# A four-layer graph network on one core: layer 0 reads the adjacency matrix by columns instead of by rows

## The chip, the core and the metric

The kernel runs on one core of a Trainium2 chip. The core has five engines that run side by side: PE (TensorE, matrix products and transposes), DVE (VectorE), ACT (ScalarE), POOL (GpSimd) and SP (SyncE, which here only issues DMAs). Each engine works through its own instructions in the order of the program and waits on semaphores for the others. The metric is the device time of one launch in microseconds (us); less is better.

## What is computed

x holds 2708 nodes of 128 features, adj is a sparse 2708 x 2708 matrix of float32 (some 17 entries a row, the diagonal always set). Four layers follow one another, each adding its result to x. Those that this change touches are the first two:

```python
# --- layer 0 ---
h = jnp.maximum(_layernorm(x), 0.0)
msg = jnp.matmul(adj.T, h)               # sum over rows of adj
inv_deg = 1.0 / adj.sum(axis=0)          # inf becomes 0
x = x + msg * inv_deg[:, None]
# --- layer 1 ---
h = jnp.maximum(_layernorm(x), 0.0)
s = h @ msg_w[:, :D].T
d = h @ msg_w[:, D:].T
messages = gelu(s[:, None, :] + d[None, :, :] + msg_b)
aggregated = jnp.einsum('ijd,ij->id', messages, adj)
new = jnp.concatenate([h, aggregated], -1) @ upd_w.T + upd_b
g = gelu(new) + h
x = x + layernorm(g) * ln_w + ln_b
# layer 2: adj @ h, then a GRU cell; layer 3: masked attention over adj
```

Layer 1 needs the messages only where adj is not zero, and the kernel uses that.

## The kernel before

The nodes lie in NT = 22 tiles of P = 128 rows (the last has TAIL = 20); GROUPS takes them four at a time, so there are six groups, the last with two tiles. For layer 1 the columns are cut into NB = 22 blocks of JB = 124, and each row's entries in a block are kept as a list of at most S = 8 values (`val`) and places (`col`).

**Layer 0** goes down adj by rows. `load_row_tile` reads 128 whole rows (1.35 MB) into one quarter of a set; two sets of four tiles are in use in turn. Each row tile is used four times:

- `list_row_tile` makes the lists on DVE: for every block a `max` (the eight largest, L283) and a `max_index` (their places, L285). Blocks that hold a part of the diagonal are first copied on POOL with the diagonal taken out (`near`). Row tiles from LATER = NT - 2 on list only those near blocks here; the others, `late_blocks`, are read again and listed three a period in layer 1 (`load_late`, `list_late`).
- `sign_sums` counts the entries of each row on ACT (L290), for a check at the end that no list ran over.
- `aggregate_rows` (PE, L297) adds h of this tile times the rows into six PSUM banks `accs`, one for each 512 columns, which hold the sums transposed and stay open over all 22 row tiles.
- `turn_blocks` transposes the tile's blocks on PE (L309). ACT copies each four of them out of PSUM, summing the columns on the way (L313), and SP writes the result to adjT in HBM, from which layer 2 reads.

The order is written out by hand (`manual_schedule`): after a set's first tile, each of the 22 steps j turns one block of the set and does a share of the products. The first four tiles of x are normalised by moments on DVE; the other 18 by sums on ACT (`sum_rows`, `sum_squares`), and a group's `normal_rows` comes one group ahead of its use.

When the last row tile is done, DVE counts the first four tiles' lists (L350 to L352), DVE and ACT copy the six banks to SBUF (L355), and five small DVE operations make the inverse degrees (L360 to L364).

**Layer 1** begins with an opening, also in an order by hand (the step list from L854 on). For each group `spread_sums` transposes the sums back (L791), `enter` adds them to x and takes moments (L800, L118 to L121), `rows` normalises (L127 to L131 on DVE, L137 on ACT), `turn_rows` transposes h (L155, L157), and `destinations` and `split_destinations` project it and split it in three bfloat16 parts (L826, L841 to L843). In between, the lists of row tiles 0, 1 and 2 pass through the steps that each tile needs: `rank` (L465), `select_rows` (DVE, L437), a shift by one row through DMA (L481), `finish_rows` (L487), `fetch` (L498), `place` (L511 to L532), `pass_on` (two DMAs, L564 and L566), `columns` (L574), `put_values` (POOL, L543).

Then `period(t)` runs for every tile: `combine` (PE, L625 and L629) builds the messages, ACT takes the Gelu, `gather` (L650) adds them up, while later tiles pass through the earlier steps. combine(0, 0) and the first gather mark the end of the opening. Layers 2 and 3 follow with code of their own.

The line that fixes the order in layer 0's inner loop is

```python
turn_blocks(gi, j)
now = len(steps) * (j + 1) // NT if gk == 4 else min(len(steps), j + 1)
```

Of the kernel before, what the change touches and what calls it, by code (L numbers as in the profile page):

```python
# [45 lines left out]
S = 8  # L46
# [14 lines left out]
def listed_layers(ctx: ExitStack, tc: tile.TileContext, x, adj, w, out, flag):  # L61
# [80 lines left out]
    def normalise(dst, src, t, k, func, name):  # L142

        rows = tiles_of(src, t, k)
        scale_rows(tiles_of(dst, t, k), rows, *factors(*moments(rows, name)), func)

# [12 lines left out]
    normalise(h, xs, 0, 4, AF.Relu, "n0")  # L159

# [6 lines left out]
    total = keep.tile([P, NT], F32, name="total")  # L167
# [27 lines left out]
    LATER = NT - 2  # L195
    AT_ONCE = 3
    late_blocks = []
    nc.gpsimd.memset(val[:, NT - 1, :, :], 0.0)
    nc.gpsimd.memset(col[:, NT - 1, :, :], 0.0)

    sumT = keep.tile([D, N], F32, name="hT1")
    hT = sumT
    with tc.tile_pool(name="l0c", bufs=1) as fix:
        offdiag = fix.tile([P, P], F32, name="offdiag")
        nc.vector.tensor_scalar(offdiag, ident, -1.0, 1.0, ALU.mult, ALU.add)
        sums = fix.tile([P, NT, len(GROUPS)], F32, name="sums")
        nc.gpsimd.memset(sums, 1.0)

        RT = NT - 4
        flat = fix.tile([P, 4, RT], F32, name="flat")
        shifts, ve, rstd, tmp = (flat[:, q, :] for q in range(4))

        def sum_rows(pool):
            for t in range(4, NT):
                junk = pool.tile([P, D], F32, name="junk")
                nc.scalar.activation(junk, xs[:, t, :], AF.Copy, accum_out=shifts[:, t - 4 : t - 3])
            nc.gpsimd.tensor_scalar(shifts, shifts, -1.0 / D, None, ALU.mult)

        def sum_squares(pool):
            for t in range(4, NT):
                junk = pool.tile([P, D], F32, name="junk")
                nc.scalar.activation(
                    junk, xs[:, t, :], AF.Square, bias=shifts[:, t - 4 : t - 3], accum_out=ve[:, t - 4 : t - 3]
                )
            nc.gpsimd.tensor_scalar(ve, ve, 1.0 / D, EPS, ALU.mult, ALU.add)
            nc.gpsimd.tensor_tensor(rstd, ve, minus_half[:, 0:RT], ALU.pow)
            nc.gpsimd.tensor_tensor(tmp, rstd, rstd, ALU.mult)
            nc.gpsimd.tensor_tensor(tmp, tmp, ve, ALU.mult)  # L230
            nc.gpsimd.tensor_scalar(tmp, tmp, -0.5, 1.5, ALU.mult, ALU.add)
            nc.gpsimd.tensor_tensor(rstd, rstd, tmp, ALU.mult)
            nc.gpsimd.tensor_tensor(shifts, shifts, rstd, ALU.mult)

        def normal_rows(g):
            t, k = GROUPS[g]
            scale_rows(tiles_of(h, t, k), tiles_of(xs, t, k), rstd[:, t - 4 :], shifts[:, t - 4 :], AF.Relu)

        with (
            tc.tile_pool(name="l0", bufs=2) as rows,  # L240
            tc.tile_pool(name="l0k", bufs=2) as pool,
            tc.tile_pool(name="l0t", bufs=8) as turned,
            tc.tile_pool(name="l0p", bufs=1, space=PSUM) as acc,
        ):
            accs = [acc.tile([P, CH], F32, name=f"acc{c}") for c in range(len(CHUNKS))]
            sets, marks = {}, {}

            def load_row_tile(n):
                gi, q, m = n // 4, n % 4, size(n)
                if q == 0:  # L250
                    sets[gi] = rows.tile([P, 4, N], F32, name="a")
                if m < P:
                    nc.gpsimd.memset(sets[gi][:, q, :], 0.0)
                nc.sync.dma_start(sets[gi][0:m, q, :], adj[n * P : n * P + m, :])

            def list_row_tile(n):

                m = size(n)
                a = sets[n // 4][:, n % 4, :]
                d0 = n * P  # L260
                b0 = d0 // JB
                b1 = (d0 + m - 1) // JB
                c0, c1 = b0 * JB, min((b1 + 1) * JB, N)
                near = pool.tile([P, 3 * JB], F32, name="near")
                nc.gpsimd.tensor_copy(near[:, 0 : c1 - c0], a[:, c0:c1])
                nc.gpsimd.tensor_tensor(
                    near[:, d0 - c0 : d0 - c0 + m], a[:, d0 : d0 + m], offdiag[:, 0:m], ALU.mult
                )
                marks[n] = pool.tile([P, P], F32, name="dg")
                nc.gpsimd.tensor_tensor(marks[n][:, 0:m], a[:, d0 : d0 + m], ident[:, 0:m], ALU.mult)  # L270

                def block(b):
                    if b0 <= b <= b1:
                        return near[:, b * JB - c0 : b * JB - c0 + width(b)]
                    return a[:, b * JB : b * JB + width(b)]

                blocks = [b for b in range(NB) if not b0 <= b <= b1] + list(range(b0, b1 + 1))
                if n >= LATER:
                    late_blocks.extend((n, b) for b in range(NB) if not b0 <= b <= b1)
                    blocks = range(b0, b1 + 1)  # L280
                for k in range(0, NB, 2):
                    for b in blocks[k : k + 2]:
                        nc.vector.max(val[:, n, b, :], block(b))  # L283
                    for b in blocks[k : k + 2]:
                        nc.vector.max_index(col[:, n, b, :], val[:, n, b, :], block(b))  # L285

            def sign_sums(n):
                m = size(n)
                sign = pool.tile([P, N], BF16, name="sign")
                nc.scalar.activation(sign, sets[n // 4][:, n % 4, :], AF.Sign, accum_out=total[:, n : n + 1])  # L290
                dg = marks.pop(n)[:, 0:m]
                nc.scalar.activation(dg, dg, AF.Copy, accum_out=own[:, n : n + 1])

            def aggregate_rows(n, ci):
                c, cw = CHUNKS[ci]
                m = size(n)
                nc.tensor.matmul(  # L297
                    accs[ci][:, 0:cw], h[0:m, n, :], sets[n // 4][0:m, n % 4, c : c + cw],
                    start=(n == 0), stop=(n == NT - 1),
                )  # L300

            def turn_blocks(gi, j):
                g0, gk = GROUPS[gi]
                i0, iw = span(g0, gk)
                k = size(j)
                p = bank("p_T")
                for q in range(gk):
                    m = size(g0 + q)
                    nc.tensor.transpose(  # L309
                        p[0:k, q * P : q * P + m], sets[gi][0:m, q, j * P : j * P + k], ident[0:m, 0:m]  # L310
                    )
                aT = turned.tile([P, CH], F32, name="aT")
                nc.scalar.activation(aT[0:k, 0:iw], p[0:k, 0:iw], AF.Copy, accum_out=sums[0:k, j, gi : gi + 1])  # L313
                nc.sync.dma_start(adjT[0:k, j, i0 : i0 + iw], aT[0:k, 0:iw])

            with tc.manual_schedule():
                for n in range(8):
                    load_row_tile(n)
                    if n == 1:
                        load_rest()  # L320
                for gi, (g0, gk) in enumerate(GROUPS):
                    steps = [(n, ci) for n in range(g0, g0 + gk) for ci in range(len(CHUNKS))]
                    ahead = gi == 0
                    for n in range(g0, g0 + gk):
                        if ahead:
                            for ci in range(len(CHUNKS)):
                                aggregate_rows(n, ci)
                        if n < 2:
                            list_row_tile(n)
                            sign_sums(n)  # L330
                            (sum_rows, sum_squares)[n](pool)
                    done = 0
                    for j in range(NT):
                        turn_blocks(gi, j)
                        now = len(steps) * (j + 1) // NT if gk == 4 else min(len(steps), j + 1)
                        for step in steps[done:now]:
                            if not ahead:
                                aggregate_rows(*step)
                        done = now
                        n = g0 + j // 5  # L340
                        if j % 5 == 1 and j // 5 < gk and n > 1:
                            list_row_tile(n)
                        if j % 5 == 3 and j // 5 < gk and n > 1:
                            sign_sums(n)
# [50 lines left out]
    with (  # L395
# [331 lines left out]
        def period(t, between=()):  # L727
# [5 lines left out]
            for k in range(GB):  # L733
# [45 lines left out]
                if k == 4:  # L779
                    load_late(t + 1)  # L780
# [957 lines left out]
```

## Time and profile before

| | us |
|---|---|
| median of 3 runs | 1064.76 (1064.54 to 1066.95) |
| the profiled execution | 1063.62 |
| its span, first to last instruction | 1061.8 |
| layer 0, to the last list on DVE | 205.3 |
| opening of layer 1, to the first gather | 205.3 to 290.5 |
| periods of layer 1, to the last gather | 290.5 to 609.0 |
| layers 2 and 3 | to the end |

Over the whole span PE is busy 87% of the time, DVE 77%, ACT 48% and POOL 43%; the mean granted TensorE clock is 0.942 of full speed. Such shares are means over stages that differ, so the tables below give busy time for stretches. Groups of instructions are given by line, engine, operation, the names of output and input, shapes and count; then busy time, the mean duration in ns, and the idle time of the engine ahead of them with what ended it. In timelines the columns are start, duration, engine, line and operation. A wait reads: engine and line that waited, for whom, total us, times, longest.

### The profile page before, as it was taken

The page shows a single profiled execution, that of the slowest core. Times are in us where ns is not written, and L with a number is a line of the kernel's source. Part 1 is how long each engine was busy: PE and PEld are TensorE (multiplying, and loading weights), DVE is VectorE, ACT ScalarE, POOL GpSimd, SP SyncE. Part 2 cuts the span into 40 slices and gives each one's busy share as a digit, 9 for nine tenths or more (in the row PEclk, how much of TensorE's full clock was granted, in tenths as well). Part 3 has the DMA queues.
Part 4 walks back from the last instruction along what each step waited for, and adds up shares of the span by engine and source line. Part 5 has one row for each costly group of instructions (what it writes and reads, how often), then busy time and mean ns, then how long its engine had stood idle before and what let it go on. Part 6 is the DMA issues. An engine that isn't in the chain of part 4 may idle for free. (4 is left out here: it accounts for less than half of the span.)

```text
span 1061.8 us, 22014 instructions
## 1 busy us (share of the span) xinstructions
PE 928.5 (87%) x7950; PEld 749.4 (71%) x7950; DVE 815.6 (77%) x2853; ACT 513.1 (48%) x1450; POOL 451.5 (43%) x486
## 2 busy tenths in 40 slices
PE   5798889944699999989999969999979999999983
PEld 2454455433599999989989924444478899989982
DVE  7999999868478777887878164656678987997793
ACT  7777778534566675666666521433322200230142
POOL 3310112022788778788978262444320200250042
PEclk9999999756699999999999978999999999999996
DMA  9888997221143333223231055566410000000000
GB/s 365 312 299 309 331 346 257 75 64 50 55 125 120 103 117 101 97 87 111 84 110 57 28 196 201 178 222 230 124 38 22 7 8 1 2 16 6 1 11 19
DMA packets 60625, 129.67 MB, mean 122 GB/s; under 512 B 11160, under 2 KB 23828, under 8 KB 57798
## 3 DMA queue, kind: packets, MB, share of 16 engines
q1 hardware_dynamic: 58690, 125.38, 34.7%
q10 hardware_dynamic: 1816, 2.80, 0.8%
q8 instruction: 64, 1.05, 0.4%
q14 instruction: 55, 0.45, 0.1%
HBM read 81.55 MB, written 30.87 MB: 106 GB/s over the span
## 5 line engine op out<-in xcount | busy, mean ns | idle before, releaser
L543 POOL TENSOR_SCALAR put<-count,line,value 128x128 f32<-128x128 f32 x176 | 198.3, 1139 | 38.9 <-DVE value L532 38.9
L984 PE MATMUL att<-hv,wt 128*128 128x129 f32 x1672 | 196.1, 278 | 8.8 <-DVE wt L954 8.7
L984 PEld LDWEIGHTS att<-hv,wt 128*128 128x128 f32 x1672 | 192.4, 194 | 11.8 <-DVE wt L954 8.6
L625 PE MATMUL p_m<-s,sel 128*128 128x128 bf16 x1452 | 161.8, 220 | 6.1 <-ACT g L637 5.9
L629 PE MATMUL p_m<-d,cols 124*128 124x128 bf16 (+1 forms) x1452 | 162.0, 220 | 0.2 <-DVE cols L574 0.2
L121 POOL TENSOR_TENSOR n_r<-n_r,minus_half 128x4 f32<-128x4 f32 (+1 forms) x31 | 46.3, 1493 | 268.2 <-DVE n_r L120 262.6
L954 DVE SCALAR_TENSOR_TENSOR wt<-row,lift,mask 128x1024 f32<-128x1024 f32 (+1 forms) x132 | 138.8, 1082 | 23.2 <-PE att L984 23.2
L297 PE MATMUL acc<-a,hs 128*128 128x512 f32 (+2 forms) x264 | 124.1, 572 | 10.9 <-ACT hs L137 10.9
L650 PE MATMUL agg<-put,g 128*128 128x128 f32 (+1 forms) x968 | 122.5, 278 | 0.0
L1123 PE MATMUL p_agg<-a,hs 128*128 128x512 f32 (+2 forms) x264 | 111.9, 567 | 11.2 <-DMA a<-adjT 6.9
L309 PEld LDWEIGHTS p_T<-ident,a 128*128 128x128 f32 x484 | 59.6, 143 | 87.4 <-ACT aT L313 40.0
L650 PEld LDWEIGHTS agg<-put,g 128*128 128x128 f32 x968 | 113.2, 192 | 0.0
L625 PEld LDWEIGHTS <-sel 128*128 128x128 bf16 x1452 | 103.7, 98 | 7.7 <-issue 7.2
L285 DVE FIND_INDEX8 col<-val,a 128x8 uint16<-128x124 f32 (+1 forms) x400 | 105.6, 272 | 0.0
L309 PE MATMUL p_T<-ident,a 128*128 128x128 f32 x484 | 81.6, 287 | 25.6 <-ACT aT L313 19.5
L629 PEld LDWEIGHTS <-cols 124*128 124x128 bf16 (+1 forms) x1452 | 102.7, 98 | 0.3 <-DVE cols L574 0.3
L552 ACT ACTIVATE put<-mine,value 128x128 f32<-128x128 bf16 x308 | 100.5, 391 | 0.0
L637 ACT ACTIVATE g<-p_m 128x512 f32<-128x512 f32 x132 | 72.7, 551 | 54.8 <-PE agg L650 41.5
L313 ACT ACTIVATE aT<-p_T 128x512 f32<-128x512 f32 (+2 forms) x132 | 71.2, 542 | 44.5 <-ACT aT L313 32.6
L283 DVE MAX8 val<-a 128x8 f32<-128x124 f32 (+1 forms) x400 | 90.5, 264 | 2.3 <-DMA a<-in_adj 2.3
L1123 PEld LDWEIGHTS p_agg<-a,hs 128*128 128x128 f32 (+1 forms) x264 | 48.6, 198 | 61.2 <-issue 52.3
L297 PEld LDWEIGHTS acc<-a,hs 128*128 128x128 f32 (+1 forms) x264 | 44.3, 201 | 26.2 <-issue 15.1
(261 smaller groups left out, 1500.3 us busy)
## 6 DMA issues: line engine op xcount, KB each, us to landing
a<-in_adj SPq DMA_DIRECT2D x21, 1354.0 KB
adjT<-aT SPq DMA_DIRECT2D x105, 256.0 KB
a<-adjT SPq DMA_DIRECT2D x20, 1280.0 KB
spread<-passed SPq DMA_DIRECT2D x22, 704.0 KB
later<-sel SPq DMA_DIRECT2D x22, 616.0 KB
row<-own_d ACTq DMA_DIRECT2D x10, 256.0 KB
later<-sel SPq DMA_DIRECT2D x22, 82.5 KB
adjT<-aT SPq DMA_DIRECT2D x21, 74.0 KB
```

Source lines behind the costliest of these rows:

```text
L283: nc.vector.max(val[:, n, b, :], block(b))
L285: nc.vector.max_index(col[:, n, b, :], val[:, n, b, :], block(b))
L297: nc.tensor.matmul(accs[ci][:, 0:cw], h[0:m, n, :], sets[n // 4][0:m, n % 4, c : c + cw], start=(n == 0), stop=(n == NT - 1),)
L309: nc.tensor.transpose(p[0:k, q * P : q * P + m], sets[gi][0:m, q, j * P : j * P + k], ident[0:m, 0:m])
L543: nc.gpsimd.tensor_scalar(st["put", 0][:, b, :], count, st["line"][:, b : b + 1], st["value"][:, b : b + 1], ALU.is_equal, ALU.mult,)
L552: nc.scalar.activation(st["put", 1][:, b - HP, :], st["mine"][:, b - HP, :], AF.Identity, scale=st["value"][:, b : b + 1])
L625: nc.tensor.matmul(p[:, b - b0, :], st["sel"][:, b, :], s3[:, q, t % 2, :], start=(q == 0), stop=False)
L629: nc.tensor.matmul(p[:, b - b0, :], st["cols"][0:kb, b, :], d3[0:kb, b, q, :], start=False, stop=(q == 2))
L650: nc.tensor.matmul(agg, g[:, b - 4 * k, :], put, start=(b == 0), stop=False)
L954: nc.vector.scalar_tensor_tensor(wt[:, 0:n], row[:, k, c : c + n], lift[:, j, k : k + 1], mask[:, j, c : c + n], op0=ALU.max, op1=ALU.mult,)
L984: nc.tensor.matmul(banks[s // 3][:, s % 3, :], wt[:, q * P : (q + 1) * P], hv[:, j, k, :], start=(v < 2 and s // 3 not in touched), stop=( ...
L1123: nc.tensor.matmul(pa[:, 0:n], h[0:k, j, :], a[0:k, j - j0, 0:n], start=(j == 0), stop=(j == NT - 1))
```

## The change

Layer 0 is rewritten; layer 1's opening loses what layer 0 now does. adj is cut into six pieces of columns (`window`: 512 to 576 columns each, overlapping so that both the 128-wide tiles and the 124-wide blocks of a piece are whole; the last has 228). A piece is read down all rows, four row tiles to a DMA, into a ring of four buffers:

```diff
+    RING = 4
+    def window(c):
+        return 4 * JB * c, min(CH * (c + 1), N)
+    def load_cut(c, s):
...
+        if gk == 4 and (c, s) != (0, 0):
+            nc.sync.dma_start(
+                a[:, :, 0 : hi - lo], adj[g0 * P : (g0 + 4) * P, lo:hi].rearrange("(t p) e -> p t e", p=P)
+            )
+            return
+        for n in range(g0, g0 + gk):
+            m = size(n)
+            nc.sync.dma_start(a[0:m, n - g0, 0 : hi - lo], adj[n * P : n * P + m, lo:hi])
```

`mask_near` (POOL) and `list_cut` (DVE) make the lists of a piece, with the same two operations a block. `work_cut` has the products, the transposes and the signs. In the products the block of adj is now the stationary operand, and h with a column of ones (129 wide) moves, so that the sums come out by nodes, with the degree in column 129. The copy of the turned blocks no longer sums:

```diff
+    def work_cut(c, s):
...
+        def products(n):
+            m = size(n)
+            for q in range(tk):
+                k, e = size(t0 + q), (t0 + q) * P - lo
+                nc.tensor.matmul(
+                    pv[0:k, q // 2, q % 2, :], a[0:m, n - g0, e : e + k], h0[0:m, n, :],
+                    start=(n == 0 and q % 2 == 0), stop=(n == NT - 1), skip_group_check=True,
+                )
...
+            aT = turned.tile([P, CH], F32, name="aT")
+            nc.scalar.copy(aT[0:k, 0 : n * iw], p[0:k, 0 : n * iw])
+            nc.sync.dma_start(
+                adjT[0:k, js[0] : js[0] + n, i0 : i0 + iw], aT[0:k, 0 : n * iw].rearrange("p (j i) -> p j i", j=n)
+            )
+            if c > 0 and todo and gk == 4:
+                products(todo.pop(0))
+        for n in todo:
+            products(n)
...
+        nc.scalar.activation(
+            sign[:, 0:whole, 0 : e1 - e0], a[:, 0:whole, e0:e1], AF.Sign, accum_out=total[:, s, c : c + 1]
+        )
```

While piece c is read, the nodes of piece c - 1 are finished: `invert` (inverse degrees, DVE), `spread` (scaling on ACT, adding to x on POOL), `sum_rows`, `sum_squares` and `normal_rows` (ACT and POOL); those of piece c - 2 are turned and projected. During piece 0 the sums, squares and normal rows of x itself for groups 1 to 5 stand there, spread over s = 0 to 4:

```diff
+    order = [(c, s) for c in range(LAST) for s in range(len(GROUPS))]
+    for i, (c, s) in enumerate(order):
+        g0, gk = GROUPS[s]
+        mask_near(c, s)
+        list_cut(c, s, g0)
...
+        work_cut(c, s)
+        if i > 0 and i - 1 + RING < len(order):
+            load_cut(*order[i - 1 + RING])
+        if c == LAST - 1:
+            load_cut(LAST, s)
+        if c == 0:
...
+        elif s == 0:
+            invert(c - 1)
+        elif s == 2:
+            spread(c - 1)
+        elif s == 3:
+            sum_rows(*GROUPS[c - 1])
+        elif s == 4:
+            sum_squares(*GROUPS[c - 1])
+        elif s == 5:
+            normal_rows(h, *GROUPS[c - 1])
+        if c > 1 and s == 0:
+            turn_rows(c - 2)
+        if c > 1 and s == 1:
+            destinations(c - 2)
+        if c > 1 and s == 3:
+            split_destinations(c - 2)
```

The last piece has buffers of its own. Its products and transposes come at once, its lists within the opening of layer 1, whose step list is now

```diff
+    enter(LAST - 1)
+    for s in range(len(GROUPS)):
+        work_cut(LAST, s)
...
+        for step, n in (
+            (list_last, 0), (count_first, 0), (rank, 0), (rows, 4), (select_rows, 0), (describe, 0), (turn_rows, 4),
+            (list_last, 1), (finish_rows, 0), (fetch_both, 0), (split_destinations, 3), (enter, 5), (rank, 1),
+            (destinations, 4), (select_rows, 1), (place, 0), (pass_on, 0), (sources, 0), (split_destinations, 4),
+            (rows, 5), (describe, 1), (list_last, 2), (turn_rows, 5), (destinations, 5), (finish_rows, 1),
+            (fetch_both, 1), (columns, 0), (split_destinations, 5), (place, 1), (rank, 2), (select_rows, 2),
+            (list_last, 3), (describe, 2), (list_last, 4), (list_last, 5), (close_lists, 0),
+        ):
+            step(n)
+        putpool = puts.enter_context(tc.tile_pool(name="l1q", bufs=2, reuse_waits="tile"))
+        for step, n in ((put_values, 0), (put_rest, 0), (finish_rows, 2)):
+            step(n)
```

Three smaller edits go with it. LATER becomes NT - 3, so that row tile 19 too is listed late, and the 20-row tile's late blocks are read by `load_wide` side by side on the partitions, so that four `max` and four `max_index` (`list_wide`) do them; small DMAs carry the results to `val` and `col`. The pools of layer 1 wait for memory tile by tile (`reuse_waits="tile"`). `project` and `mix` take their PSUM banks from the pool of two (`bank`) in place of one bank that they shared with `rank` and `pass_on`.

## The prediction

> **What bounds the kernel now.** I read the mean clock and span first, then busy time by 50 us stretches, which splits the run into its layers. Columns are busy us and instruction counts of each engine, the granted TensorE clock, the DMA share and GB/s.
>
> ```profile
> 0.00:50.00 50.00, 34.49 (x132) 19.49 (x132) 44.04 (x298) 36.55 (x129) 18.32 (x43) 0.97 0.90 345
> 50.00:100.00 50.00, 40.92 (x189) 23.95 (x188) 50.00 (x340) 38.99 (x96) 6.85 (x16) 0.96 0.86 296
> 100.00:150.00 50.00, 44.36 (x211) 26.34 (x210) 50.00 (x339) 40.19 (x97) 6.33 (x15) 1.00 0.96 341
> 150.00:200.00 50.00, 43.74 (x189) 23.94 (x188) 50.00 (x340) 37.14 (x97) 8.60 (x16) 1.00 0.66 221
> 200.00:250.00 50.00, 30.24 (x119) 19.35 (x117) 34.09 (x132) 20.85 (x64) 10.60 (x16) 0.56 0.25 75
> 250.00:300.00 50.00, 29.40 (x305) 26.32 (x306) 32.46 (x79) 26.85 (x79) 30.14 (x33) 0.73 0.16 48
> 300.00:350.00 50.00, 49.90 (x741) 49.16 (x740) 36.55 (x82) 33.62 (x105) 41.84 (x46) 1.00 0.38 119
> ```
>
> To 205 us (layer 0) DVE is full, with DMA and PE not far below. From 205 to 290 us no engine is full: this is the opening of layer 1. Then PE is full. Groups of the first 200 us, kept apart by shape, say what fills DVE, and what ACT does beside it:
>
> ```profile
> L285 DVE FIND_INDEX8 col<-val,a 128x8 uint16<-128x124 f32 x374 | 99.3, 273 | 0.0
> L283 DVE MAX8 val<-a 128x8 f32<-128x124 f32 x375 | 86.0, 265 | 2.3 <-DMA a<-in_adj 2.3
> L313 ACT ACTIVATE aT<-p_T 128x512 f32<-128x512 f32 x105 | 62.0, 593 | 35.0 <-ACT aT L313 23.1 <-issue 6.7 <-PE p_T L309 5.2
> L290 ACT ACTIVATE sign<-a 128x2708 bf16<-128x2708 f32 x21 | 51.5, 2452 | 5.5 <-DMA a<-in_adj 5.5
> ```
>
> The lists (top eight of each block of 124 columns, and their places) never wait. In order of time a pair of blocks repeats each 0.89 us (198.54, 199.43, 200.32), so a block costs 0.445 us. The landmarks come from the timelines of DVE and PE: last list, rank(0), combine(0, 0), first gather:
>
> ```profile
> 205.04 0.26 DVE L285 FIND_INDEX8 col<-val,near 128x8 uint16<-128x104 f32 x1
> ...
> 216.77 0.22 PE L465 MATMUL p_r<-rows_n,before 128*128 128x22 bf16 x1
> ...
> 273.90 0.53 PE L625 MATMUL p_m<-s,sel 128*128 128x128 bf16 x3
> ...
> 290.54 2.00 PE L650 MATMUL agg<-put,g 128*128 128x128 f32 x16
> ```
>
> Between these, the waits from 205 to 290 us name the loop of layer 0's result being normalised, group by group:
>
> ```profile
> PE p_h L155 <- ACT hs L137: 29.2, 5, 6.9
> POOL n_r L121 <- DVE n_r L120: 21.5, 4, 9.6
> ```
>
> The chain of waits itself holds only the last microsecond, so I judge by stage. Gathers run from 290.5 to 609 us on a full PE. The change alters little there, so I take what the first gather gains as what the run gains.
>
> **What the Trainium skill says.** "ScalarE: Activation LUTs", What ACT_TABLE_LOAD costs: an ACTIVATE takes 186 ns + 0.833 ns an element, 93 ns more for each pointer operand, and neighbours overlap by about 93 ns. For 2708 elements that is 2.44 us; the trace has 2.452. "TensorE: Matmul & The Clock Gate", Architectural detail: TensorE's queue can pull a weight load ahead of running matmuls. The layer 3 products agree: 196 us of matmuls beside 192 us of loads. "DMA: Bandwidth & Descriptors", How a descriptor splits into AXI transactions: a read that doesn't start on 256 bytes fetches from the boundary below. The new pieces start so (a row is 10,832 bytes, a piece some 2.1 KB); no transfer of before shows it.
>
> **The change, part by part.**
>
> *Lists.* Before: 20 tiles of 22 blocks and 3 near ones, 443 x 0.445 = 197 us, which is 7.5 to 205.3. After, pieces 0 to 4 hold 19 x 20 + 1 = 381 blocks, 169.5 us. The last piece's 42 (18.7 us) go into the opening, where DVE is busy 67 of 100 us. Late blocks in layer 1 stay at three a period (40 for 41), and the short tile's 21 become 4 wide ones.
>
> *Start.* The first piece is 0.26 MB for 1.35, so DVE starts near 5.2 us for 7.5; the four rows' factors cost 1.3 as now.
>
> *Added on DVE.* invert, three small operations like L361 to L364 (0.65 us) x4; split_destinations (L841, 0.68) x3: 4.6 us. Unhindered, piece 4's lists end at 5.2 + 1.3 + 169.5 + 4.6 = 180.6.
>
> *PE.* Products now hold the block of adj as weights and move 129 columns. The same shape runs in layer 3, two records each, and the old cadence gives the transposes:
>
> ```profile
> 899.78 20.15 PE L984 MATMUL att<-hv,wt 128*128 128x129 f32 x179
> ```
> ```profile
> 176.85 0.60 PE L309 MATMUL p_T<-ident,a 128*128 128x128 f32 x4
> ...
> 177.28 1.02 PE L297 MATMUL acc<-a,hs 128*128 128x512 f32 x2
> ```
>
> 20.15 / 179 x 2 = 0.225 us a product; 177.28 - 176.85 = 0.43 for four transposes, 0.11 each. A full piece of four tiles is 16 x 0.335 = 5.4 us against DVE's 16 x 0.445 = 7.1. PE stays below. Alternation with transposes isn't shown: from 0.225 if weight loads hide, to 0.45 at half clock. I take 0.225.
>
> *ACT, first column.* All normalising of x falls into column 0. By cadence: sums 18 x 0.30, squares 18 x 0.39, rows 22 x 0.41; per piece 4 copies x 0.50 and a sign over 2048 elements, 1.9 (skill, confirmed). Pieces 0 to 3 end on ACT at about 23.5, 32, 39.5 and 46 us when it starts at 8.4. SP issues the load three pieces ahead after the adjT writes of a piece, so the load of (1, 0) is issued at about 43 and lands near 48; DVE is through column 0 at 40.7. Stall 7 us, bounds 0 to 12. Behind that load on SP stand the next writes, and behind their buffers ACT and PE. Later columns cost ACT 30 us against DVE's 35.
>
> *DMA.* Reads 29.5 MB for five columns and 2.5 for the last (overlapping windows), x 1.4, weights 1.2, writes 27.7: 62.2 MB by then.
>
> ```profile
> q1 hardware_dynamic: 25174, 59.91, 84.0%
> ```
> ```profile
> 610.00:620.00 10.00, 5.79 (x12) 2.60 (x12) 5.83 (x29) 4.22 (x10) 3.82 (x4) 0.51 0.93 332
> ```
>
> 59.9 MB took 84% of 200 us: 357 GB/s when busy. Layer 2's reads of 2 KB runs give 332/0.93 = 357. Unaligned reads may lose about 3% overall (estimate from the skill's 256 bytes: half of one on 2.1 KB, on half the traffic): about 345 GB/s, 180 us. That is nearly DVE's time, so I add 4 us for collisions, bounds 0 to 20. Lists end at 180.6 + 7 + 4 = 192 for 205.3.
>
> *To rank(0).* Gone: copies of the sums, transposing them back, degrees. Instead enter(4) 3.8 (0.65 + 1.12 + 2.0 by L800, L118, L119), eight blocks 3.6, counts 1.4 (L350, L352): 8.8, at 201 (11.5 before). enter(4) waits for PE's products; everything on DVE stands behind. PE's last piece, 44 x 0.335 plus a turn and destinations, 17 us, stands ahead of rank(0), but PE can be two or three pieces ahead, so it ends about together. Cover gone, it costs up to 8 us.
>
> *To combine(0, 0).* Five of the six enter-and-rows rounds leave this stretch or shrink (about 4.1 us of DVE each, with waits on POOL and ACT). DVE then holds: rank twice 0.8, factors 2.0, select twice 3.2, describe 0.7, blocks of groups 1 and 2 7.1, finish twice 3.2, splits 1.4, enter(5) 2.6, place 3.7, sources 1.1, columns 0.95: 26.8. Waits: 1 for later's DMA (4.6 us after the selection at 268.7), 1.5 for project, 3 for ACT's Gelu table (1.28) ahead of describe(1): 32 for 57.1. So 233.
>
> *To the first gather.* DVE: place(1), rank(2), select, describe, finish and 18 blocks of groups 3 to 5, 16 us; then put_values(0) on POOL, 7.6 by L543, whose buffers lie where the last piece lay. Behind it on POOL: put_values(1). 23 for 16.6: at 256.
>
> Sum: 290.5 - 256 = 34.5 us. project and mix in other banks may give 2 in layer 1, and the 17 or so small transfers of the wide lists on SP may take 3; layer 2's first load may move by 3 either way with the layout. I take these as nothing. The profiled execution took 1063.6 (span 1061.8): 1029.1. The median, 1064.76, lies 1.1 above: **1030 us**.
>
> **Rivals.**
> 1. *DMA takes over layer 0.* For: shares of 0.9 to 1.0 already, both directions in 2 KB runs now. Against: layer 2's 357 GB/s. At 300 GB/s lists end at 207, a gain of about 20: 1045.
> 2. *No stall in column 0, no collisions, opening without waits.* ACT may overlap better and DMA keep up: 11 us of layer 0 and 5 of the opening more: 1014.
> 3. *PE becomes the bound, slower.* Pieces 0 to 4 have 440 products and 440 transposes. If weight loads show between transposes, PE ends these at 8 + 48 + 8 + 440 p, the second 8 being turns and destinations. From p = 0.37 us the whole gain is gone (end at 227 for 192). At 0.42: 249, so 1087. For: weights change at every product, and matmuls took twice as long at clock 0.5 in the opening. Against: 0.225 in layer 3, clock 0.97 to 1.00 in layer 0.
> That the change doesn't do what it says isn't likely: the new order is written out by hand.
>
> **How the numbers follow.** Forecast 0.55 (its own range 1020 to 1040), rival 1 0.17, rival 2 0.13, rival 3 0.13, no change 0.02. Range 1010 to 1050: it takes in the first three and leaves rival 3 and the edge out. 0.3% (3 us) is about what this measurement can tell from no change. Faster 0.85, same 0.02, slower 0.13.
>
> **What would show it.** Right: DVE full to about 192 with one hole near 41 to 48 us before the second column; rank(0) near 201, combine(0, 0) near 233, first gather near 256, and the last gather as much earlier as the first. Wrong: PE full in layer 0 and DVE waiting for loads whose buffers PE holds; DMA at share 1.0 with DVE waiting through all columns; first gather early, but layer 1 longer.

## The result, and the profile after

The changed kernel is slower by 0.8%: median 1071.88 us (1070.95 to 1077.13) beside 1064.65 us (1064.40 to 1066.95) for the kernel before, ratio 1.0077, 95% interval 1.0056 to 1.0099. The forecast was 1030 us. The profiled execution took 1074.57 us, its span 1072.8. By the landmarks of the forecast:

| us from the start | before | forecast | after | late by, and new in this step |
|---|---|---|---|---|
| start of the last list of layer 0 on DVE | 205.0 | 192 | 213.3 | 21.3 |
| rank(0) on PE | 216.8 | 201 | 240.8 | 39.8, new 18.5 |
| combine(0, 0) | 273.9 | 233 | 271.3 | 38.3, regained 1.5 |
| first gather | 290.5 | 256 | 291.4 | 35.4, regained 2.9 |
| first to last gather takes | 318.5 | 318.5 | 326.1 | 7.6 |
| last gather to the end of the span takes | 452.8 | 452.8 | 455.3 | 2.5 |

35.4 + 7.6 + 2.5 = 45.5, and 1029.1 + 45.5 = 1074.6. The loss has three places: layer 0 itself, the step from the last list to rank(0), and layer 1. The opening after rank(0) went as forecast.

The table of stretches of the changed kernel (columns as before: busy us and counts of PE, PEld (PE's weight loads), DVE, ACT, POOL, then clock, DMA share, GB/s):

```profile
0.00:50.00 50.00, 26.22 (x171) 24.20 (x172) 37.49 (x247) 34.75 (x116) 22.79 (x74) 0.90 0.67 219
50.00:100.00 50.00, 45.77 (x383) 42.91 (x381) 41.18 (x277) 39.50 (x93) 11.77 (x36) 1.00 0.97 326
100.00:150.00 50.00, 43.69 (x376) 42.01 (x377) 43.95 (x294) 39.36 (x86) 12.41 (x34) 1.00 0.93 307
150.00:200.00 50.00, 42.60 (x347) 40.94 (x345) 47.53 (x318) 37.17 (x84) 12.13 (x31) 0.93 0.92 317
200.00:250.00 50.00, 39.10 (x236) 27.85 (x234) 23.69 (x125) 29.25 (x85) 14.28 (x42) 0.84 0.43 140
250.00:300.00 50.00, 25.73 (x279) 22.86 (x280) 40.67 (x142) 22.87 (x72) 24.01 (x30) 0.65 0.24 77
```

Before, DVE was busy 50.00 of 50 us from 50 to 200. Now it is busy 41 to 48, and no engine is full: PE 43 to 46, ACT 37 to 40, DMA 0.92 to 0.97. What DVE waited for up to 215 us (engine and line that waited, for whom: total us, times, longest):

```profile
DVE val L349 <- DMA a<-in_adj: 19.0, 4, 10.7
...
DVE val L349 <- POOL near L332: 10.1, 7, 5.5
```

These two lines are almost all of layer 0's lateness. The forecast had 180.6 us of unhindered work when the first list starts at 5.2. It starts at 8.51: 180.6 + 3.3 + 19.0 + 10.1 = 213.0, for the measured 213.3. The block's price of 0.445 us was right.

Now the landmarks. DVE's timeline shows the last list and the first instruction behind rank(0), PE's shows the first and the last operation of the last piece and rank(0):

```profile
213.27 0.28 DVE L351 FIND_INDEX8 col<-val,near 128x8 uint16<-128x124 f32 x1
...
214.89 0.18 DVE L423 RECIPROCAL inv_deg<-sums 128x4 f32<-128x4 f32 x1 [1.34 <-PE sums L368]
...
241.02 0.18 DVE L648 CAST ends<-p_r 128x22 bf16<-128x22 f32 x1 [17.69 <-PE p_r L647]
```
```profile
215.66 0.66 PE L382 MATMUL p_T<-ident,z 128*128 128x128 f32 x4 [0.81 <-ACT aT L386]
...
239.31 1.55 PE L368 MATMUL sums<-h,z 128*128 128x129 f32 x8
240.80 0.19 PE L647 MATMUL p_r<-rows_n,before 128*128 128x22 bf16 x1
```

The bracket on the third DVE line is the idle time before it and its releaser: 17.69 us for rank(0). PE starts on the last piece only at 215.66, after DVE's last list, and needs 25 us for it; rank(0) stands behind all of that. For part of this time the granted clock was half (0.50 from 220 to 224 us): the first two sets of eight products, with their transposes, took 5.34 and 5.04 us, the third, at clock 1.00, took 3.66.

In layer 1, SP's timeline and the one long wait of PE:

```profile
523.86 0.76 SPq L641 DMA_DIRECT2D val<-tops  x1
...
532.53 0.72 SPq L641 DMA_DIRECT2D col<-tops_at  x1
533.36 0.44 SPq L746 DMA_DIRECT2D passed<-where_T  x1
536.20 0.36 SPq L748 DMA_DIRECT2D spread<-passed  x1
```
```profile
542.47 0.50 PE L811 MATMUL p_m<-d,cols 124*128 124x128 bf16 x3 [6.94 <-DVE cols L756]
```

Twelve small transfers of the wide list hold SP for 9.5 us; behind them stand the two transfers of pass_on, whose columns PE's combine needs.

### The profile page after: what moved, and what is told of

The parts are those of the page before. It is cut to its first block, busy times and chain, and to the rows that moved or that the text cites. A ratio compares the mean times of both kernels' runs of the same rounds, so it can differ in the third digit from the quotient of the medians.

```text
span 1072.8 us, 23407 instructions
## 1 busy us (share of the span) xinstructions
PE 930.4 (87%) x8632; PEld 813.9 (76%) x8632; DVE 793.9 (74%) x2742; ACT 516.6 (48%) x1427; POOL 472.1 (44%) x596
## 5 line engine op out<-in xcount | busy, mean ns | idle before, releaser
L1124 PE MATMUL att<-hv,wt 128*128 128x129 f32 x1672 | 193.4, 276 | 9.0 <-DVE wt L1094 9.0
L1124 PEld LDWEIGHTS att<-hv,wt 128*128 128x128 f32 x1672 | 189.8, 192 | 11.9 <-DVE wt L1094 8.9
L121 POOL TENSOR_TENSOR n_r<-n_r,minus_half 128x4 f32<-128x4 f32 (+1 forms) x27 | 39.1, 1447 | 241.0 <-DVE n_r L120 237.3
L1263 PE MATMUL p_agg<-a,hs 128*128 128x512 f32 (+2 forms) x264 | 111.0, 563 | 12.5 <-DMA a<-adjT 12.5
L368 PE MATMUL sums<-h,a 128*128 128x129 f32 (+1 forms) x880 | 119.6, 284 | 0.0
L382 PE MATMUL p_T<-ident,a 128*128 128x128 f32 (+1 forms) x440 | 73.9, 291 | 44.1 <-ACT aT L386 32.8
L368 PEld LDWEIGHTS sums<-h,a 128*128 128x128 f32 (+1 forms) x880 | 111.3, 200 | 0.8
L382 PEld LDWEIGHTS p_T<-ident,a 128*128 128x128 f32 (+1 forms) x440 | 54.6, 148 | 52.5 <-ACT aT L386 36.4
L349 DVE MAX8 val<-a 128x8 f32<-128x124 f32 x342 | 79.4, 274 | 19.0 <-DMA a<-in_adj 19.0
L351 DVE FIND_INDEX8 col<-val,a 128x8 uint16<-128x124 f32 x342 | 92.3, 283 | 0.0
L386 ACT COPY aT<-p_T 128x512 f32<-128x512 f32 (+2 forms) x122 | 66.1, 565 | 42.8 <-PE p_T L382 35.0
```

What stands on the lines that cost most here:

```text
L349: nc.vector.max(val[0:m, n, b, :], v)
L351: nc.vector.max_index(col[0:m, n, b, :], val[0:m, n, b, :], v)
L368: nc.tensor.matmul(pv[0:k, q // 2, q % 2, :], a[0:m, n - g0, e : e + k], h0[0:m, n, :], start=(n == 0 and q % 2 == 0), stop=(n == NT - 1), ...
L382: nc.tensor.transpose(p[0:k, i * iw + q * P : i * iw + q * P + m], a[0:m, q, e : e + k], ident[0:m, 0:m])
L1124: nc.tensor.matmul(banks[s // 3][:, s % 3, :], wt[:, q * P : (q + 1) * P], hv[:, j, k, :], start=(v < 2 and s // 3 not in touched), stop=( ...
L1263: nc.tensor.matmul(pa[:, 0:n], h[0:k, j, :], a[0:k, j - j0, 0:n], start=(j == 0), stop=(j == NT - 1))
```

## The experiments

All start from the changed kernel and were compared with the kernel before on the same chip (its median was 1064.2 to 1064.9 in every group). Landmarks come from one profiled execution each. How well they repeat is seen where layer 0 is the same code: lists end at 213.3, 213.6 and 212.0 in the changed kernel, wide_after and by_width. The last piece is the same code in the changed kernel and wide_after: rank(0) follows the last list after 27.5 and 25.5 us there, and in wide_after the granted clock stayed at 1.00 through it.

| label | median us | ratio to before, 95% | last list | rank(0) | first gather | last gather |
|---|---|---|---|---|---|---|
| the change | 1071.9 | 1.0056 to 1.0099 | 213.3 | 240.8 | 291.4 | 617.5 |
| x_once | 1070.0 | 1.0035 to 1.0065 | 210.4 | 236.5 | 287.5 | 612.2 |
| loads_first | 1070.7 | 1.0032 to 1.0082 | 211.8 | 238.6 | 289.7 | 613.9 |
| wide_after | 1064.5 | 0.9987 to 1.0015 | 213.6 | 239.1 | 291.0 | 606.4 |
| rank_early | 1075.1 | 1.0054 to 1.0117 | 219.8 | 234.1 | 298.6 | 622.9 |
| no_writes | 1068.2 | 1.0023 to 1.0048 | 210.0 | 235.9 | 287.9 | 612.3 |
| by_width | 1069.1 | 1.0019 to 1.0055 | 212.0 | 234.3 | 285.8 | 610.4 |
| open_early | 1062.6 | 0.9969 to 1.0001 | 211.3 | 222.6 | 280.3 | 604.9 |
| combo | 1055.3 | 0.9863 to 0.9923 | 211.9 | 234.6 | 285.8 | 602.2 |
| queues | 1062.0 | 0.9942 to 0.9984 | 198.7 | 229.9 | 281.9 | 604.8 |
| combo_early | 1049.1 | 0.9810 to 0.9867 | 212.1 | 222.0 | 277.6 | 593.6 |
| all | 1044.5 | 0.9773 to 0.9831 | 198.7 | 213.9 | 273.0 | 588.1 |
| all_stats | 1041.6 | 0.9736 to 0.9806 | 199.0 | 215.2 | 271.8 | 587.1 |

### x_once: the start

The first copy of x (L79) is issued a second time at L461; SP waits for the first to land. The edit takes the second away.

```diff
-    nc.vector.memset(xs[:, NT - 1, :], 0.0)
-    nc.sync.dma_start(xs[:, 0:4, :], x[0 : 4 * P, :].rearrange("(t p) d -> p t d", p=P))
     load_cut(0, 0)
```

> The first rows of x are loaded once and not twice. Theory A (layer 0's lateness is a sum of single waits, each of which shifts all that follows): the queue no longer waits 2.5 us for the first copy, the first list comes at 5.5 us for 8.5 and ACT's first row near 10 for 13.4; the load of piece (1, 0) goes out 3 us earlier, lists of piece 4 end 3 us earlier (210.5), median near 1069. Rival B (transfers bound columns 1 to 4, so an earlier start is spent waiting there): lists of piece 4 end within 1 us of 213.5, median 1071 to 1073.

The first list starts at 5.33 for 8.51, the lists end at 210.4, 2.9 us earlier, and the first gather comes 3.9 earlier: theory A in layer 0. The whole run gains less than its own interval can show.

### loads_first: the hole before the second piece

```diff
-        work_cut(c, s)
         if i > 0 and i - 1 + RING < len(order):
             load_cut(*order[i - 1 + RING])
+        work_cut(c, s)
```

> Each load of a piece is issued ahead of the four adjT writes of the piece at hand, not behind them. Theory A: the load of (1, 0) then waits only for the signs and products of (0, 2) (about 45 us) and goes out at 45.5 for 50.0; the 10.7 us hole on DVE shrinks to about 6, the 2.4 and 5.3 us waits for loads at 66 and 142 us go; lists of piece 4 end 5 to 8 us earlier, median 1064 to 1067. Rival B (transfers bound): the hole in column 0 shrinks but waits for loads grow later by as much; lists end at most 2 us earlier, median 1070 to 1072.

The lists end 1.5 us earlier, no more than such a landmark varies by itself. This is rival B's number, but not its reason: DVE's waits for loads didn't grow later, they fell from 19.0 to 7.1 us. Its waits for near masks rose from 10.1 to 14.3 us instead, and those for PE's sums from 1.3 to 6.2.

### no_writes: are the transfers the bound?

```diff
-            nc.sync.dma_start(
-                adjT[0:k, js[0] : js[0] + n, i0 : i0 + iw], aT[0:k, 0 : n * iw].rearrange("p (j i) -> p j i", j=n)
-            )
...
-            nc.sync.dma_start(a[:, 0:whole, 0:n], adjT[:, j0 : j0 + whole, c : c + n])
+            nc.sync.dma_start(
+                a[:, 0:whole, 0:n], adj[j0 * P : (j0 + whole) * P, c : c + n].rearrange("(t p) e -> p t e", p=P)
+            )
```

> Leaves out the 27.7 MB of adjT writes (the transposes and the copies out of PSUM stay); layer 2 reads the same number of bytes from adj itself in their place, so it works on adj and not on its transpose. Only layer 0 is looked at. Theory D (transfers set the pace of layer 0 from piece 1 on, share 0.92 to 0.97 at 307 to 326 GB/s): with 34.6 MB left, DVE no longer waits for loads after column 0 and the lists of piece 4 end between 188 and 198 us for 213.5. Rival E (PE, ACT and the turns of their queues set the pace; ACT's copies wait 29 us for PE and PE 33 for ACT): waits move from loads to near masks and PE, lists end no earlier than 207.

Theory D, which was mine, fell. Two of the stretches of this kernel, and what DVE then waits for, from its timeline and its list of waits:

```profile
50.00:100.00 50.00, 46.60 (x383) 43.73 (x382) 43.39 (x293) 38.63 (x93) 12.86 (x41) 0.99 0.54 171
100.00:150.00 50.00, 44.89 (x388) 43.43 (x389) 47.95 (x320) 40.17 (x87) 11.21 (x31) 1.00 0.57 182
```
```profile
DVE val L349 <- POOL near L332: 14.9, 6, 8.3
...
DVE inv_deg L420 <- PE sums L368: 7.3, 2, 6.5
...
DVE val L349 <- DMA a<-in_adj: 4.0, 1, 4.0
```

The DMA share fell from 0.95 to 0.55, and the lists ended 3.3 us earlier. DVE's waits for loads fell from 19.0 to 4.0, but waits for near masks grew from 10.1 to 14.9 and for PE's sums from 1.3 to 7.3. So one wait takes another's place. POOL's timeline around the 8.3 us says how:

```profile
136.83 0.29 POOL L332 TENSOR_TENSOR near<-a,offdiag 128x48 f32<-128x48 f32 x1
155.20 1.28 POOL L438 TENSOR_TENSOR xs<-xs,part_x 128x512 f32<-128x512 f32 x1 [18.08 <-ACT part_x L437]
156.41 0.30 POOL L331 COPY near<-a 128x124 f32<-128x124 f32 x1
156.78 0.34 POOL L332 TENSOR_TENSOR near<-a,offdiag 128x76 f32<-128x76 f32 x1
```

POOL stood for 18.08 us at `spread`'s addition, which waits for ACT's `part_x`; the mask that DVE wanted came behind it, and DVE went on at 157.16. ACT's copies in turn wait for PE (32.1 us up to 215 us), and PE's transposes for ACT's copies (32.1 us). DVE can't run further ahead than this chain lets it. The Trainium skill says in "TensorE: Matmul & The Clock Gate", Architectural detail, that ACT and DVE work strictly first in, first out, and POOL likewise within each of its cores; this trace agrees, as the mask (156.41) ran only behind the addition that had waited 18.08 us.

### queues: the orders themselves

Four edits of order: those of x_once and loads_first, the fourteen weight transfers (123.6 to 132.5 us on SP) moved to the end of layer 1, and

```diff
-        mask_near(c, s)
+        if i < 6:
+            mask_near(c, s)
...
             list_cut(c, s, n)
+        if 5 <= i < len(order) - 1:
+            mask_near(*order[i + 1])
```

with eight buffers for masks in place of six.

> Four edits of layer 0's queues and nothing else: rows of x loaded once; loads ahead of the adjT writes; the fourteen weight transfers (8.9 us of SP in piece 2) moved to the end of layer 1; on POOL the near masks of the next piece ahead of the normalising of this one, from piece 1 on. Theory E (layer 0 is late by single waits in the queues' orders; DVE, PE, ACT and DMA all have room): the waits of 3, 5.9 and up to 10 us on near masks go, lists of piece 4 end between 196 and 204 us for 213.5, first gather 10 to 16 us earlier, median 1057 to 1062. Rival H (after column 0, which ACT ends at 62 us, PE has no more room): DVE waits at invert for PE instead, lists end no earlier than 207, median 1065 to 1069.

The lists end at 198.7, 14.6 us earlier with nearly the same traffic (62 MB by 213 us in both): theory E. But the first gather came only 9.5 us earlier. DVE's waits in this kernel, and the line after its last list:

```profile
DVE inv_deg L425 <- PE sums L370: 16.9, 4, 6.5
...
DVE val L351 <- DMA a<-in_adj: 4.0, 1, 4.0
...
DVE val L351 <- POOL near L334: 2.4, 4, 1.6
```
```profile
205.33 0.18 DVE L425 RECIPROCAL inv_deg<-sums 128x4 f32<-128x4 f32 x1 [6.33 <-PE sums L370]
```

29.1 us of waits for loads and masks have become 6.4, and 1.3 us for PE's sums 16.9: PE is now the last, as rival H had it, 7 us behind DVE, though the lists end 8 us before rival H's 207. Median 1062.0, at the upper end of E's range.

### wide_after: the small transfers

```diff
-            for i, (b, k) in enumerate(pieces):
-                for dst, src in ((val, tops), (col, tops_at)):
...
+                if k in (1, 3) and t == WIDE_AT + 1:
+                    keep_wide(3 * (k == 3))
                 if k == 3 and c:
                     columns(t + 1)
```

`keep_wide` issues six of the twelve transfers; DVE's part stays where it was.

> The twelve small transfers of the wide list are issued in two halves in the period after, each behind that period's own transfers, not all ahead of pass_on. Theory A: the 6.9 us wait of PE for columns at 542 us goes, first gather stays at 291.4, last gather comes near 610 for 617.5, median near 1065. Rival: layer 1 is longer for other reasons (lists of the short tile, clock), the wait moves to another place: last gather 615 to 617, median 1070 to 1072.

First gather 291.0, median 1064.5, as theory A had them; the last gather, at 606.4, came even 3.6 us sooner. First to last gather takes 315.4 us, 10.7 less than in the changed kernel and 3.1 less than before the change.

### rank_early and open_early: what holds rank(0), and what holds the rest

rank_early moves the first tiles' lists, rank(0) and select_rows(0), with its shift on SP, behind the second of the last piece's six sets. To find memory for `sel0` it makes the scratch outputs `sign` and `junk` single.

```diff
+    for n in range(4):
+        list_cut(LAST, 0, n)
...
     for s in range(len(GROUPS)):
         work_cut(LAST, s)
+        if s == 1:
+            p = bank("p_r0")
+            nc.tensor.matmul(p[:, 0:NB], before, rows_n[:, 0, :], start=True, stop=True)
...
+            compare(sel0, ends4, ALU.is_ge)
```

> The lists of the last piece's first four tiles, their counts, rank(0) and select_rows(0) stand after the second of the last piece's six sets of products, not behind all six. Theory A (what holds the opening is that rank(0) stands behind 25 us of PE work): rank(0) near 226 for 240.8, DVE's 17.7 us wait falls to 3 and the rest is filled, first gather near 280 for 291.4, median 1059 to 1063. Rival C (PE's own work ahead of fetch(0), to 241 us, holds the opening whatever the place of rank(0)): rank(0) as early, but the first gather at most 5 us earlier, median 1067 to 1070.

A miss: 1075.1. Two things spoil it. Layer 0 ended 6.5 us later: with one `junk` buffer ACT's sums and squares drag (last section). open_early below, whose `sign` is single too and whose `junk` has two, ends its lists at 211.3. And though rank(0) came 14.3 us after the last list and not 27.5, the opening didn't follow. From this kernel's timeline of all engines:

```profile
246.65 0.82 PE L383 MATMUL p_T<-ident,z 128*128 128x128 f32 x4
...
248.94 0.18 DVE L1034 TENSOR_SCALAR lost<-own 128x22 f32<-128x22 f32 x1 [11.74 <-ACT dg L413]
...
249.32 1.65 ACT L137 ACTIVATE hs<-xs,n_r 128x128 f32<-128x128 f32 x4
```

The rows of group 4 (ACT, L137) were due at 237.2, when DVE had their factors. They ran at 249.32, because in ACT's order they stand behind the last piece's copies and signs, which follow PE's transposes. describe(0), the split of tile 0's values that fetch(0) needs, stands behind the rows. DVE's 11.7 us wait, at the check that no list ran over (`lost`), is for L413, ACT's last operation of the last piece. So I moved what follows on the other engines too:

```diff
     for s in range(len(GROUPS)):
         work_cut(LAST, s)
+        if s == 0:
+            rows(4)
         if s == 1:
...
+            nc.scalar.copy(parts[0], val[:, 0, :, :])
...
+            for n in range(4, 8):
+                list_cut(LAST, 1, n)
+            nc.vector.tensor_tensor(sel0, sel0, later, ALU.subtract)
```

> As in rank_early, but what follows rank(0) on ACT, POOL and SP goes ahead too: rows(4) stands after the first set of the last piece, rank(0), select_rows(0), its shift, describe(0), the second lists and finish_rows(0) after the second; only one buffer is single (the signs' output), sums and squares keep two. Theory A2 (the last piece's work stands ahead of the opening in the order of PE, ACT and SP all three, so moving rank(0) alone gained nothing): fetch(0) comes right after the last piece's work, near 242 for 250, first gather 5 to 9 us earlier, median 1063 to 1067. Rival G (the opening is held by a chain that starts at the end of that work, transposing the normalised group 4 and projecting it): first gather at most 3 us earlier, median 1069 to 1073.

rank(0) at 222.6, the first fetch at 237.9 for 250.2, first gather 11.1 us earlier (2.0 of it in layer 0), median 1062.6, a little better than A2's range. The last piece's work stood ahead of the opening on PE, ACT and SP at once. rank_early had moved the chain past it on PE and SP (its shift left SP at 236.4 for 243.8) and left ACT's part behind it; open_early moves that too, with the steps on DVE and POOL that follow. Counted from the last list, the first gather took 78.1 us in the changed kernel, 78.8 in rank_early and 68.9 in open_early, about 9 us less. What each of the moves is worth wasn't measured.

### by_width: why the last piece costs PE 25 us

```diff
+            if c == LAST and gk == 4:
+                for n in range(g0, g0 + gk):
+                    products(n, (js[0] - t0,))
+                todo = []
```

> In the last piece the products of the 128-wide tile are issued four in a row, and then those of the 20-wide tile, in place of one of each in turn. Theory F (a product costs 0.36 us there and not 0.2225 because the width of the weights changes at every product, so that the next load isn't hidden): 40 products come down to about 0.23 us each, the last piece's work on PE from 25 to about 20 us, rank(0) and the first gather 4 to 6 us earlier, median 1066 to 1068. Rival (a 20-wide product costs that by itself, or the clock does it): no change, 1071 to 1073.

PE's timeline for one set of eight products, first in the changed kernel, then in by_width:

```profile
226.54 0.60 PE L382 MATMUL p_T<-ident,z 128*128 128x128 f32 x4
226.97 0.71 PE L368 MATMUL sums<-h,z 128*128 128x129 f32 x4
227.62 0.60 PE L382 MATMUL p_T<-ident,z 128*20 128x128 f32 x4
228.06 2.21 PE L368 MATMUL sums<-h,z 128*128 128x129 f32 x12
230.20 0.66 PE L382 MATMUL p_T<-ident,z 128*128 128x128 f32 x4
```
```profile
222.46 0.60 PE L382 MATMUL p_T<-ident,z 128*128 128x128 f32 x4
222.90 1.06 PE L368 MATMUL sums<-h,z 128*128 128x129 f32 x8
223.79 0.60 PE L382 MATMUL p_T<-ident,z 128*20 128x128 f32 x4
224.32 1.06 PE L368 MATMUL sums<-h,z 128*20 128x129 f32 x8
225.31 0.66 PE L382 MATMUL p_T<-ident,z 128*128 128x128 f32 x4
```

A product is two records (the view names a merged line by its first, so the x12 holds both widths). In turn, six take 230.20 - 228.06 = 2.14 us, 0.357 each; by width four take 223.79 - 222.90 = 0.89, 0.22 each, and four of the narrow ones 0.99, 0.25 each. The granted clock was 1.00 in both stretches, so neither half of the rival explains it. A set of the last piece falls from 3.66 to 2.85 us, as theory F had it. rank(0) comes 22.3 us after the last list for 27.5, but only about 3 of these 5.2 us belong to the widths: by_width ran its last piece at clock 1.00 throughout, as wide_after did, where rank(0) came after 25.5.

The same lines narrow theory F's reason. Transposes of 20-wide weights follow 128-wide products at the usual pace (223.79 - 222.90 = 0.89 for eight records), though the width changes. Four such transposes ahead of 20-wide products take 224.32 - 223.79 = 0.53 us, though it doesn't change; ahead of 128-wide products they take 228.06 - 227.62 = 0.44. So about 0.1 us is added at a change into or out of 20-wide products, from transposes too. A change of width alone doesn't cost it, and what does isn't shown.

### combo, combo_early, all, all_stats: do the gains add?

combo is x_once, loads_first, wide_after and by_width together; combo_early adds open_early; all adds the two further edits of queues; all_stats takes groups 4 and 5 of x in piece 0 by moments on DVE in place of sums on ACT.

> Together: rows of x loaded once, loads ahead of the writes, the wide list's transfers in the period after, the last piece's products by width. If the gains add (4.5, 1.5, 7.6 in the profile, and 4 to 6 expected for the widths): median 1053 to 1057, faster than the kernel before by 0.7 to 1.0%. Rival (the early gains are eaten by transfers, the last by what else the opening waits for): 1060 to 1064, no change against before.

> combo and open_early together. If the last piece's work on PE is shorter by 5 us and the opening no longer stands behind it, both gains add: first gather near 275 to 278 (285.8 in combo, 280.3 in open_early), median 1045 to 1049. If they are the same gain in two forms: first gather 279 to 281, median 1049 to 1053.

> combo_early with the weight transfers moved and the near masks ahead. Theory E: another 6 to 12 us of layer 0, median 1036 to 1043. Rival H (PE has no more room in layer 0): within 3 us of combo_early.

> all, and in piece 0 the moments of x for groups 4 and 5 on DVE (which waits there for the load of (1, 0)) in place of sums and squares on ACT. ACT ends piece 0 about 4 us earlier; if ACT's piece 0 is what the whole of layer 0 stands behind, lists of piece 4 end 3 to 4 us earlier than in all and the median is lower by as much; if DVE or PE set the pace after it, no change or a loss of up to 3.

combo: 1055.3, inside the first range, but the landmarks say that only two of the four gains add. Its first gather, 285.8, is that of by_width alone, and from there to the last gather it takes 316.4 us, as wide_after does (315.4). Its lists end at 211.9, only 1.4 us earlier than in the changed kernel, where x_once and loads_first promised 2.9 and 1.5: DVE's waits for loads fall from 19.0 to 9.8, but those for near masks rise from 10.1 to 14.9 and those for PE's sums from 1.3 to 5.4. That the median was forecast rightly is luck in this part.

combo_early: 1049.1, on the border of the two ranges; its first gather, 277.6, lies in the first one's. Against open_early it comes 2.7 us earlier, so the two gains add in part. all: 1044.5, another 4.6 us, less than theory E asked for (its interval overlaps that of combo_early at the edge). Its lists end 13.4 us earlier, nearly all of what queues gained, so the moved weight transfers and the order of the masks bring it; the two were not run apart. The first gather gains only 4.6, mainly since PE is last there too (DVE waits 6.3 us for its sums after the last list). all_stats: 1041.6, but its lists end no earlier than in all and the two intervals overlap, so the last 3 us are not shown. all and all_stats beat the kernel before by 2.0 and 2.3%, where the change alone lost 0.8%.

## Why the prediction was wrong

**The steps that failed.** Two steps hold some 40 of the 45.5 us.

"Lists end at 180.6 + 7 + 4 = 192": 213.3. Each term of waiting was too small, and one was missing. The start (5.2, measured 8.5) overlooked that x is copied twice. The stall after column 0 (7) came to 10.7 at once and 2.4 behind it, since ACT began its rows 5 us later than I had put it and the load of (1, 0), the first of piece 1, left SP at 50.0 for 43. "4 us for collisions" stood for transfers in each other's way. The other 5.9 us of waits for loads (0.6 at 129 us, 5.3 at 142) came instead behind the fourteen weight transfers that hold SP from 123.6 to 132.5: in combo_early 4.6 us of this are left at 136 us, in all, with these transfers moved, none. The waits for near masks, 10.1 us, weren't in the sum: I had priced what POOL does, not what stands ahead of it. As I read it the root is one: I took DVE for the only full engine and added the rest as small corrections, where the new order ties four queues together at 0.74 to 0.97 of their time. That is why mending one wait alone gained little (loads_first, no_writes): the next queue's wait took its place.

"PE's last piece ... stands ahead of rank(0), but PE can be two or three pieces ahead, so it ends about together. Cover gone, it costs up to 8 us": it cost 17.7. PE was not ahead at all; DVE waited 1.3 us for its sums at the end of piece 4. It had waited 32.8 us for ACT's copies by then. And the last piece took it 25 us for 17: about 5 of these 8 us because a set of eight products and their transposes took 3.66 for the 2.68 that 0.335 each gives, and about 3 because the clock was at half for the first two sets. Counted from the last list, the first gather comes 4.4 us earlier in by_width (3.6 against wide_after, where the clock was the same) and 9.2 in open_early.

**A term of the right kind, mis-sized.** The "17 or so small transfers of the wide lists on SP may take 3": with their order mended, the stretch between the gathers is 10.7 us shorter. The 2 us that other banks for project and mix "may give" are likely there: 315.4 us for 318.5, and PE's waits for the bank that they shared with rank (3.0 us before, all for `ends`) don't appear in wide_after. No run took the banks alone.

**What held.** A block at 0.445 us. Four products and a turn in pieces 0 to 4 repeat every 1.33 us, as 0.225 and 0.11 say. From rank(0) to combine(0, 0) 30.5 us for 32, and from there to the first gather 20.1 for 23: what left the opening was worth what the forecast gave for it. Layers 2 and 3 moved by 2.5, inside the 3 allowed.

**The rivals.** Rival 1 (transfers take over) had the rate about right, 307 to 326 GB/s from 50 to 200 us for its 300, and the cause wrongly: with the writes gone the lists end 3.3 us earlier, and in queues, with nearly all bytes there, 14.6. Rival 2 (no stall, no collisions) had it the wrong way round. Rival 3 had the sign. Its price for a product (0.37 and more) was met only in the last piece, not in pieces 0 to 4. No rival held that work of the old stage, on three engines, could stand ahead of the new one.

No order tried here reaches the forecast of 1030: the kernel with all repairs, at 1041.6, is 12 us above it, and its lists end at 199.0 for 192.

What stays open: the moved weight transfers and the order of the near masks were never run apart, nor the moves that open_early makes on ACT, POOL and DVE. How all_stats differs from all isn't settled. That PE is what holds layer 0 in queues is read from its waits; no run made PE's work in pieces 0 to 4 smaller.

## What to carry to other kernels

When a stage is rewritten so that several engines come near their limits, don't add a stall or two to the busiest engine: follow, for each engine and queue, what stands ahead of the instruction that the busiest one waits for, small transfers and helper copies too. At the seam between two stages, list what the old stage still has to issue on every engine before the new stage's first chain; here moving that chain past the shares of PE and SP gained nothing, and moving it past ACT's too gained 9 us. Gains measured one at a time need not add, since the wait that one edit removes can come back on another queue. Edits that hardly touch the work were worth more here than the change: 2.6% between the changed kernel and all (1071.9 to 1044.5).

## What the hardware showed that I had not expected

- Products whose stationary operand changes width each time (128 columns, then 20) cost 0.357 us each, for 0.22 to 0.25 with the widths grouped, at clock 1.00 in both. The Trainium skill, "TensorE: Matmul & The Clock Gate", Step-by-step: what each phase is for, says that a weight load is pulled ahead of running products when their row groups don't conflict or when it goes to the background weight buffer; with equal widths the trace agrees (eight records in 0.89 us, 0.11 each). That with alternating products the load is not hidden is my reading of the times, not shown by itself; the change of width alone is not the reason, as by_width's transposes show.
- A DMA share of 0.92 to 0.97 at 307 to 326 GB/s was no bound: with 27 of 62 MB gone (no_writes) the lists ended 3.3 us earlier, and with nearly all of them there but the queues reordered (queues) 14.6.
- With a single scratch buffer for outputs that nobody reads (rank_early), ACT was through its first run of sums and squares in piece 0 12.5 us after the start of the sign ahead of it (17.77 to 30.25), with two buffers after 9.9 us (18.03 to 27.93, the changed kernel). It is the buffer of the sums: in open_early only the sign's is single, and it took 10.0 us (17.88 to 27.86).
- A transfer from SBUF to SBUF of 20 rows held SP for 0.72 us (0.76 the first), twelve of them for 9.5 us.
